# A recurrent layer on one core: four groups of seven transposed by DMA instead of three, with a shared reciprocal square root and copies split between two engines

## The chip, the cores and the metric

The kernel runs on one core of a Trainium2 chip. The metric is the device time of one execution in microseconds. Five instruction streams work side by side: TensorE (PE, with its weight loads PEld), VectorE (DVE), ScalarE (ACT), GpSimd (POOL) and SyncE (SP, which here only issues DMAs). Each runs its own instructions in order; between streams they wait on semaphores. L1101 means line 1101 of the kernel.

## The reference

Two layers over 3327 nodes with 256 features, each a graph attention followed by a feed-forward part. Layer 0 has a two-head attention and a mixture of 16 experts. Layer 1 has a one-head attention and the part that matters here, a recurrence of 30 steps over all rows:

```python
def step(h, _):
    h = h + 0.01 * jnp.tanh(h)
    h = h * jax.nn.sigmoid(h)
    h = _layernorm(h, ln_w, ln_b)
    h = jnp.einsum('bsc,dc->bsd', h, W) + b
    return (h, None)
x, _ = jax.lax.scan(step, x, None, length=N_ITERS)     # N_ITERS = 30
```

`_layernorm` subtracts the mean of a row, multiplies by 1/sqrt(variance + 1e-5) and applies `ln_w` and `ln_b`. Rows don't depend on each other, steps do.

## The kernel before

Rows are held in 26 tiles of 128 rows, features along the free dimension, in one SBUF tensor `x`. Two attentions, the experts and the second attention come first (about 1080 us); the change is in the recurrence behind them.

**Groups.** The 26 tiles make seven groups (`COUNT`): positions 0 to 5 have four tiles, position 6 has two. 30 steps of seven groups are 210 groups, numbered by `at`; the position is `at % 7`. As seven is odd, a position has an even number in one step and an odd one in the next. Within one step the groups are independent; group `at` needs what group `at - 7` has left in `x`.

**Stages of a group**, each a method of `Group`:

- `tanh` (L1046, ScalarE): `th = tanh(hs / 100)`; `hs` is the group's part of `x`, scaled by 100.
- `add` (L1049, GpSimd): `th = th + hs`.
- `silu` (L1053, ScalarE): `z = silu(th / 100)`.
- `measure` (L1058, L1061, VectorE): mean and variance of every row of `z`, by `bn_stats` and `bn_aggr`, one instruction a tile.
- `invert` (L1066, L1067, GpSimd): variance plus epsilon, then to the power -0.5. The mean is never subtracted from `z`; it has been taken out of the weights `wc` beforehand.
- The transpose of `z`, since the product contracts over features. There are two ways. `turn_here`: TensorE transposes 128 x 128 blocks into PSUM (L1077, eight for a group of four tiles) and ScalarE copies them to SBUF (L1079, two for a group of four tiles). `turn_away`: ScalarE splits every float into its two 16-bit halves (L1086, one copy for the group), a DMA writes these to a DRAM buffer `apart` (L1087), and a DMA of the transposing kind reads them back turned (L1091). Both DMAs are issued by SP. The positions in `AWAY = (1, 3, 5)` go this way.
- `product` (L1101, TensorE): `po = zT x wc`, 16 matrix products in two passes by four tiles, into one of two PSUM buffers `po`.
- `evict` (L1111, VectorE): `hs = po * r + bb`, one instruction a tile; `r` is the result of `invert`. In the last step it also adds the layer's input (L1119, with `old`, loaded back from DRAM by SP) and writes the output.

**Order.** The order is written out by hand, a software pipeline: iteration `at` works on groups of different ages, and `put` keeps the instructions of each engine in that order from the second step on. The loop is

```python
on(at - 1, Group.evict)
on(at + 3, Group.invert)
on(at + 4, Group.silu)
on(at + 2, lambda g: g.away or g.turn_here())
on(at + 4, lambda g: g.away and g.turn_away())
on(at + 4, Group.measure)
on(at + 6, Group.tanh)
on(at + 5, Group.add)
on(at, Group.product)
```

So on TensorE, an iteration is the transposes of the group two ahead (if it is turned there) and then a product; on VectorE, the eviction of the group behind and then the measurement of the group four ahead; on GpSimd, an inversion and an addition; on ScalarE, `silu`, copies, `tanh`. A group's state goes round in seven iterations: `evict` and the next step's `tanh` in one, `add` in the next, `silu` in the one after that, and the product four iterations later.

**Buffers.** `po` has two (a product waits until the group two before it has been evicted). `wide` tiles (`th`, `z`) have four, `narrow` ones eight. The halves and the transposed result of `turn_away` use buffers of the pool `steps`, two each, and `apart` has two.

Of the kernel before, what the change touches and what calls it, by code (L numbers as in the profile page):

```python
# [11 lines left out]
F32 = mybir.dt.float32  # L12
I32 = mybir.dt.int32
I16 = mybir.dt.int16
BF16 = mybir.dt.bfloat16
FP8 = mybir.dt.float8e4
AF = mybir.ActivationFunctionType
ALU = mybir.AluOpType
# [3 lines left out]
P = 128  # L22
ALPHA = 0.2
EPS = 1e-5
N_STEPS = 30
S = 100.0
G = 4
MOST = 6
# [3 lines left out]
def gat_moe_gat_recurrent_ffn(ctx: ExitStack, tc: tile.TileContext, a: dict, out: bass.AP):  # L32
    nc = tc.nc
    N, D = a["x"].shape
    KD = D // P
    NT = (N + P - 1) // P
    NP = NT * P
    PAIRS = NT // 2
# [25 lines left out]
    const = ctx.enter_context(tc.tile_pool(name="const", bufs=1))  # L64
# [32 lines left out]

    ident = const.tile([P, P], F32, name="ident")
    make_identity(nc, ident)
    neg_half = const.tile([P, MOST], F32, name="neg_half")  # L100
    nc.vector.memset(neg_half, -0.5)


# [80 lines left out]
    class Scores:  # L184


        def __init__(self, pool, heads, s=None):
            self.s = pool.tile([P, NT, 2, heads], F32, name="s") if s is None else s
            self.row = pool.tile([P, NT, heads], F32, name="row")
            self.full = pool.tile([P, NT, heads], F32, name="full")  # L190
            self.part = pool.tile([P, NT, heads], F32, name="part")
            self.minus = pool.tile([P, NT, heads], F32, name="minus")
# [113 lines left out]
    graph = ctx.enter_context(tc.tile_pool(name="graph", bufs=1))  # L306
    adj_pairs = graph.tile([P, PAIRS, NP], BF16, name="adjT")
    adjT = adj_pairs.bitcast(FP8).rearrange("p c (i b) -> p c i b", b=2)
# [37 lines left out]
    dram = ctx.enter_context(tc.tile_pool(name="dram", bufs=1, space=bass.MemoryType.DRAM))  # L346
# [35 lines left out]
    with ExitStack() as moe:  # L382
# [542 lines left out]
        bb = rec.tile([P, D], F32, name="bb")  # L925
# [18 lines left out]
    steps = ctx.enter_context(tc.tile_pool(name="steps", bufs=2))  # L944
# [73 lines left out]
    with ExitStack() as st:  # L1018
        ps_t = st.enter_context(tc.tile_pool(name="ps3t", bufs=2, space=PSUM))
        turns = cycle((ps, ps_t))  # L1020
        ps_o = st.enter_context(tc.tile_pool(name="ps3o", bufs=2, space=PSUM))
        last_p = st.enter_context(tc.tile_pool(name="last", bufs=2))

        apart = [dram.tile([G * P, 2, D], I16, name=f"apart{q}") for q in range(2)]
        wide = st.enter_context(tc.tile_pool(name="wide", bufs=4))
        narrow = st.enter_context(tc.tile_pool(name="narrow", bufs=8))

        AWAY = (1, 3, 5)
        COUNT = len(groups)
        LAST = N_STEPS * COUNT  # L1030

        class Group:

            def __init__(self, at):
                self.at = at
                self.ts = groups[at % COUNT]
                self.n = len(self.ts)
                self.hs = x[:, self.ts[0] : self.ts[0] + self.n, :]
                self.away = at % COUNT in AWAY

            def put(self, ins):
                return tc.keep_in_program_order(ins) if self.at >= COUNT else ins

            def tanh(self):
                self.th = wide.tile([P, G, D], F32, name="wth")[:, : self.n, :]
                self.put(nc.scalar.activation(self.th, self.hs, AF.Tanh, scale=1.0 / S))  # L1046

            def add(self):
                self.put(nc.gpsimd.tensor_tensor(self.th, self.th, self.hs, ALU.add))  # L1049

            def silu(self):
                self.z = wide.tile([P, G, D], F32, name="wz")[:, : self.n, :]
                self.put(nc.scalar.activation(self.z, self.th, AF.Silu, scale=1.0 / S))  # L1053

            def measure(self):
                stats = narrow.tile([P, G, 6], F32, name="stats")
                for j in range(self.n):
                    self.put(nc.vector.bn_stats(stats[:, j, :], self.z[:, j, :]))  # L1058
                self.v = narrow.tile([P, G, 2], F32, name="v")
                for j in range(self.n):  # L1060
                    self.put(nc.vector.bn_aggr(self.v[:, j, :], stats[:, j, :]))  # L1061

            def invert(self):
                self.r = narrow.tile([P, G], F32, name="rr")
                r = self.r[:, : self.n]
                self.put(nc.gpsimd.tensor_scalar(r, self.v[:, : self.n, 1], EPS, None, op0=ALU.add))  # L1066
                self.put(nc.gpsimd.tensor_tensor(r, r, neg_half[:, : self.n], ALU.pow))  # L1067

            def turn_here(self):
                pool = next(turns)  # L1070
                zT = steps.tile([P, G, KD, P], F32, name="zT")
                for c in range(self.n // 2):
                    pt = pool.tile([P, 2, KD, P], F32, name="bank")
                    for j in range(2):
                        for k in range(KD):
                            tc.keep_in_program_order(
                                nc.tensor.transpose(pt[:, j, k, :], self.z[:, 2 * c + j, k * P : (k + 1) * P], ident)  # L1077
                            )
                    self.put(nc.scalar.copy(zT[:, 2 * c : 2 * c + 2, :, :], pt))  # L1079
                self.zT = lambda j, k: zT[:, j, k, :]  # L1080

            def turn_away(self):
                n = self.n
                parts = steps.tile([P, G, 2, D], I16, name="th")[:, :n]
                here = apart[self.at % COUNT // 2 % 2][: n * P]
                self.put(nc.scalar.copy(parts, self.z.bitcast(I16).rearrange("p j (d b) -> p j b d", b=2)))  # L1086
                nc.sync.dma_start(  # L1087
                    here.rearrange("(j p) b d -> p j (b d)", p=P), parts.rearrange("p j b d -> p j (b d)")
                )
                zT = steps.tile([P, KD, G * P], F32, name="z")  # L1090
                nc.sync.dma_start(  # L1091
                    zT.bitcast(I16)[:, :, : n * 2 * P], here.rearrange("t b d -> (t b) d"), transpose=True
                )
                self.zT = lambda j, k: zT[:, k, j * P : (j + 1) * P]

            def product(self):
                self.po = ps_o.tile([P, G, D], F32, name="po")
                for j in range(self.n):
                    for k in range(KD):
                        tc.keep_in_program_order(  # L1100
                            nc.tensor.matmul(  # L1101
                                self.po[:, j, :], lhsT=self.zT(j, k), rhs=wc[:, k, :],
                                start=(k == 0), stop=(k == KD - 1),
                            )
                        )

            def evict(self):
                ts, n = self.ts, self.n
                for j in range(n):
                    self.put(  # L1110
                        nc.vector.scalar_tensor_tensor(  # L1111
                            self.hs[:, j, :], self.po[:, j, :], self.r[:, j : j + 1], bb, op0=ALU.mult, op1=ALU.add
                        )
                    )
                if self.at >= LAST - COUNT:
                    here = slice(ts[0] * P, (ts[-1] + 1) * P)
                    old = last_p.tile([P, G, D], F32, name="old")
                    nc.sync.dma_start(old[:, :n, :], kept[here, :].rearrange("(t p) d -> p t d", p=P))
                    nc.vector.scalar_tensor_tensor(  # L1119
                        self.hs, self.hs, 1.0 / S, old[:, :n, :], op0=ALU.mult, op1=ALU.add  # L1120
                    )
                    move_pairs(out, self.hs, ts[0] // 2, (ts[-1] + 1) // 2, True)

        live = {}

        def on(at, *what):
            if 0 <= at < LAST:
                if at not in live:
                    live[at] = Group(at)
                for w in what:  # L1130
                    w(live[at])

        for at in range(-6, LAST + 2):
            on(at - 1, Group.evict)
            live.pop(at - 1, None)
            on(at + 3, Group.invert)
            on(at + 4, Group.silu)
            on(at + 2, lambda g: g.away or g.turn_here())
            on(at + 4, lambda g: g.away and g.turn_away())
            on(at + 4, Group.measure)  # L1140
            on(at + 6, Group.tanh)
            on(at + 5, Group.add)
            on(at, Group.product)
# [49 lines left out]
```

## Time and profile before

| | us |
|---|---|
| median of 3 runs | 1873.88 (1872.47 to 1874.83) |
| profiled execution, its time | 1875.77 |
| profiled execution, its span | 1874.0 |
| TensorE busy in the span | 1815.3 (97%), mean granted clock 0.992 |
| VectorE, ScalarE, GpSimd busy | 1281.8, 1177.1, 936.9 |

The instructions of the recurrence between 1200 and 1800 us, from the groups by line and shape:

| line | engine | what | mean us of one |
|---|---|---|---|
| L1046 | ScalarE | tanh, four tiles / two | 1.06 / 0.64 |
| L1053 | ScalarE | silu, four tiles / two | 1.05 / 0.62 |
| L1079 | ScalarE | copy of two transposed tiles | 0.58 |
| L1086 | ScalarE | copy of the halves of four tiles | 1.90 |
| L1049 | GpSimd | addition, four tiles / two | 2.37 / 1.28 |
| L1066 | GpSimd | variance plus epsilon | 0.23 |
| L1067 | GpSimd | power, 4 columns / 2 | 1.04 / 0.72 |
| L1058 | VectorE | bn_stats, one tile | 0.41 |
| L1061 | VectorE | bn_aggr, one tile | 0.16 |
| L1111 | VectorE | eviction, one tile | 0.48 |

How to read it: a mean is from an instruction's start to its end, and instructions that follow each other on one engine overlap at their ends, so four of 0.41 us take 1.40. A matmul record shows about 0.38 us, yet sixteen of them take 3.46 us from start to start of what follows; the chain of waits shows these true lengths. "Idle before" is the time that an engine stood still ahead of an instruction, with what ended the wait. In the chain of waits, lines stand in order of time, and only what sets the end is in it.

### The profile page before, as it was taken

How to read it: one execution, taken by the hardware profiler on the slowest of the kernel's cores; microseconds unless marked ns; L12 is line 12 of the kernel's file. 1: busy time of each engine (PE TensorE's matmuls, PEld its weight loads, DVE VectorE, ACT ScalarE, POOL GpSimd, SP SyncE). 2: the span in 40 equal slices, each digit the busy share in tenths (PEclk: the TensorE clock that was granted, in tenths of full speed). 3: DMA queues.
4: the chain of work that ended last, by engine and by line, in shares of the span. 5: the costliest groups of instructions: out<-in, count | busy, mean ns of one | idle time of the engine just before them, and what ended most of it. 6: DMA issues, size and time to landing. Idle time of an engine off the chain costs nothing.

```text
span 1874.0 us, 32159 instructions
## 1 busy us (share of the span) xinstructions
PE 1815.3 (97%) x11204; PEld 1658.8 (89%) x11204; DVE 1281.8 (68%) x3829; ACT 1177.1 (63%) x1487; POOL 936.9 (50%) x864
## 2 busy tenths in 40 slices
PE   6999999999999998999999979999999999999997
PEld 6999999998999997788888868888888888888886
DVE  6888888842222222666767678888888888888887
ACT  2877777631111111655555578888888888888884
POOL 3010212255333331100000079999999999999994
PEclk9999999999999999999999989999999999999999
DMA  8887260179999885300000045545554555554556
GB/s 175 113 126 96 53 99 23 59 237 300 344 336 338 298 273 183 106 13 18 22 13 17 16 110 133 124 127 122 124 124 124 124 127 122 125 122 124 124 130 197
DMA packets 379919, 255.04 MB, mean 136 GB/s; under 512 B 240917, under 2 KB 339532, under 8 KB 379754
## 3 DMA queue, kind: packets, MB, share of 16 engines
q1 hardware_dynamic: 363634, 220.08, 43.0%
q0 software_dynamic: 11440, 28.09, 8.6%
q10 hardware_dynamic: 4680, 4.76, 0.8%
q8 instruction: 92, 1.51, 0.3%
q14 instruction: 73, 0.60, 0.1%
HBM read 168.19 MB, written 77.01 MB: 131 GB/s over the span
## 4 chain that ended last, share of the span: by engine, by line
PE 67%; issue 10%; POOL 6%; DVE 5%; DMA 4%; ACT 1%; SPq 0%; POOLq 0%; DVEq 0%; ACTq 0%
PE po L1101 34%; PE acc L286 25%; PE bank L1077 5%; POOL given L855 2%; POOL rb L761 2%; DVE pT L281 2%; DMA given<-wh,to 2%; DMA old<-kept 1%; DMA wh<-in_w_dram 1%; PE bank L835 1%; POOL wth L1049 1%; PE acc L163 1%; PE bank L526 1%; PE bank L148 0%; DMA lists<-pair,ati 0%
## 5 line engine op out<-in xcount | busy, mean ns | idle before, releaser
L276 ACT ACTIVATE e<-rb,minus,full 128x384 f32<-128x384 f32 (+3 forms) x494 | 402.4, 824 | 189.2 <-DVE pT L281 172.4
L1049 POOL TENSOR_TENSOR wth<-wth,x 128x1024 f32<-128x1024 f32 (+1 forms) x210 | 464.8, 2214 | 17.2 <-ACT wth L1046 17.2
L281 DVE SCALAR_TENSOR_TENSOR pT<-e,part,adjT 128x384 f32<-128x384 f32 (+3 forms) x494 | 374.7, 761 | 135.8 <-PE acc L286 120.4
L1111 DVE SCALAR_TENSOR_TENSOR x<-po,rr,bb 128x256 f32<-128x256 f32 x780 | 322.9, 475 | 99.4 <-PE po L1101 63.3
L1101 PE MATMUL po<-wc,zT 128*128 128x256 f32 x1680 | 384.2, 380 | 3.2 <-DVE x L1111 3.2
L1101 PEld LDWEIGHTS po<-wc,zT 128*128 128x128 f32 x1680 | 313.4, 191 | 43.1 <-ACT wz L1053 2.2
L1101 PE MATMUL po<-wc,z 128*128 128x256 f32 x1440 | 325.6, 379 | 0.0
L286 PE MATMUL acc<-wh,pT 128*128 128x129 f32 x2704 | 309.8, 276 | 2.1 <-DVE pT L281 2.1
L286 PEld LDWEIGHTS acc<-wh,pT 128*128 128x128 f32 x2704 | 305.0, 192 | 2.7 <-DVE pT L281 2.5
L1101 PEld LDWEIGHTS po<-wc,z 128*128 128x128 f32 x1440 | 271.3, 190 | 35.7
L286 PE MATMUL acc<-s_wh,pT 128*128 128x257 f32 x1352 | 295.8, 382 | 2.4 <-DVE pT L281 2.4
L286 PEld LDWEIGHTS acc<-s_wh,pT 128*128 128x128 f32 x1352 | 257.6, 191 | 40.4 <-DVE pT L281 3.8
L1058 DVE BATCH_NORM_STATS2 stats<-wz 128x6 f32<-128x256 f32 x780 | 274.4, 413 | 27.5 <-ACT wz L1053 27.3
L1053 ACT ACTIVATE wz<-wth 128x1024 f32<-128x1024 f32 (+1 forms) x210 | 208.0, 990 | 82.7 <-POOL wth L1049 82.4
L121 POOL TENSOR_TENSOR rstd<-ve,neg_half 128x4 f32<-128x4 f32 (+3 forms) x28 | 30.4, 1087 | 441.4 <-DVE ve L119 290.4
L1046 ACT ACTIVATE wth<-x 128x1024 f32<-128x1024 f32 (+1 forms) x210 | 209.8, 999 | 26.7 <-DVE x L1111 22.7
L1067 POOL TENSOR_TENSOR rr<-rr,neg_half 128x4 f32<-128x4 f32 (+1 forms) x210 | 208.2, 992 | 17.5
L1086 ACT COPY th<-wz 128x2048 int16<-128x2048 int16 x90 | 170.9, 1899 | 1.8
L881 ACT ACTIVATE e<-bank 128x512 f32<-128x512 f32 x61 | 36.4, 597 | 196.2 <-PE bank L835 188.8
L885 DVE TENSOR_TENSOR pT<-e,bank 128x512 f32<-128x512 f32 x61 | 41.9, 687 | 166.8 <-PE bank L835 166.7
L835 PEld LDWEIGHTS bank<-hT,wh 128*128 128x128 f32 x1280 | 149.3, 192 | 5.2 <-ACT hT L827 1.4
L835 PE MATMUL bank<-hT,wh 128*128 128x128 f32 x1280 | 150.5, 275 | 2.6 <-DMA wh<-in_w_dram 2.6
(195 smaller groups left out, 1636.3 us busy)
## 6 DMA issues: line engine op xcount, KB each, us to landing
wh<-in_w_dram SPq DMA_DIRECT2D x120, 512.0 KB
apart<-th SPq DMA_DIRECT2D x90, 512.0 KB
first_set<-in_w_dram SPq DMA_DIRECT2D x63, 512.0 KB
in_bytes<-in_adj_dram POOLq DMA_DIRECT2D x3, 2496.0 KB, 28.3
x<-in_x_dram SPq DMA_DIRECT2D x6, 512.0 KB
kept<-x SPq DMA_DIRECT2D x8, 384.0 KB
old<-kept SPq DMA_DIRECT2D x6, 512.0 KB
out_dram<-x SPq DMA_DIRECT2D x6, 512.0 KB
```

The costliest lines, as they stand in the source:

```text
L276: nc.scalar.activation(e[:, : n * P], rb[:, : n * P], AF.Relu, scale=sc.full[:, j, h : h + 1], bias=sc.minus[:, j, h : h + 1],)
L281: masked = nc.vector.scalar_tensor_tensor(pT[:, : n * P], e[:, : n * P], sc.part[:, j, h : h + 1], adjT[:, j // 2, ts[0] * P : (ts[-1] + 1 ...
L286: nc.tensor.matmul(po[c], lhsT=pT[:, c * P : (c + 1) * P], rhs=wh[:, j, h, :], start=(j == 0 and c % per_bank == 0), stop=(j == NT - 1), s ...
L835: nc.tensor.matmul(p[:, f, :], lhsT=w[:, k, f * P : (f + 1) * P], rhs=hT[:, k, :], start=(k == 0), stop=(k == KD - 1),)
L1046: self.put(nc.scalar.activation(self.th, self.hs, AF.Tanh, scale=1.0 / S))
L1049: self.put(nc.gpsimd.tensor_tensor(self.th, self.th, self.hs, ALU.add))
L1053: self.put(nc.scalar.activation(self.z, self.th, AF.Silu, scale=1.0 / S))
L1058: self.put(nc.vector.bn_stats(stats[:, j, :], self.z[:, j, :]))
L1067: self.put(nc.gpsimd.tensor_tensor(r, r, neg_half[:, : self.n], ALU.pow))
L1086: self.put(nc.scalar.copy(parts, self.z.bitcast(I16).rearrange("p j (d b) -> p j b d", b=2)))
L1101: nc.tensor.matmul(self.po[:, j, :], lhsT=self.zT(j, k), rhs=wc[:, k, :], start=(k == 0), stop=(k == KD - 1),)
L1111: nc.vector.scalar_tensor_tensor(self.hs[:, j, :], self.po[:, j, :], self.r[:, j : j + 1], bb, op0=ALU.mult, op1=ALU.add)
```

## The change

- `AWAY` is `(1, 2, 4, 5)`: four positions are turned by DMA, 0, 3 and 6 on TensorE.
- `turn_away` is cut in two. `send_away` makes the halves and writes them to DRAM, at the old place. `take_back` issues the transposing DMA one iteration later; both DMAs are kept in program order, so the write of the next group stands ahead of the transpose of this one on SP's queue.
- In `send_away`, for the odd positions (1 and 5), ScalarE copies the halves of three tiles and VectorE those of the fourth. VectorE's copy stands ahead of the group's measurement.
- `invert` is done for two groups at once, by the odd-numbered one of a pair (`at` even, `at + 1`): one L1066 and one L1067 over the columns of both.
- The buffers of the halves (three) and of the transposed result (five) are cut from the space of the adjacency `adjT`, which the second attention reads last; `apart` has four.

```diff
-    neg_half = const.tile([P, MOST], F32, name="neg_half")
+    neg_half = const.tile([P, 2 * G], F32, name="neg_half")
...
-        apart = [dram.tile([G * P, 2, D], I16, name=f"apart{q}") for q in range(2)]
+        apart = cycle([dram.tile([G * P, 2, D], I16, name=f"apart{q}") for q in range(4)])
+        space = graph.tile([P, PAIRS, NP], BF16, name="adjT").rearrange("p c n -> p (c n)").bitcast(F32)
+        spaces = [space[:, i * G * D : (i + 1) * G * D] for i in range(8)]
+        room_parts, room_back = cycle(spaces[:3]), cycle(spaces[3:])
...
-        AWAY = (1, 3, 5)
+        AWAY = (1, 2, 4, 5)
...
-            def measure(self):
+            def measure(self, other):
+                first = self.at % 2 == 0
+                if first:
+                    self.v = narrow.tile([P, 2 * G, 2], F32, name="v")
+                    self.r = narrow.tile([P, 2 * G], F32, name="rr")
+                    self.c = 0
+                else:
+                    self.v, self.r, self.c = other.v, other.r, other.n
...
             def invert(self):
-                self.r = narrow.tile([P, G], F32, name="rr")
-                r = self.r[:, : self.n]
-                self.put(nc.gpsimd.tensor_scalar(r, self.v[:, : self.n, 1], EPS, None, op0=ALU.add))
-                self.put(nc.gpsimd.tensor_tensor(r, r, neg_half[:, : self.n], ALU.pow))
+                if self.at % 2:
+                    n = self.c + self.n
+                    r = self.r[:, :n]
+                    self.put(nc.gpsimd.tensor_scalar(r, self.v[:, :n, 1], EPS, None, op0=ALU.add))
+                    self.put(nc.gpsimd.tensor_tensor(r, r, neg_half[:, :n], ALU.pow))
...
-            def turn_away(self):
+            def send_away(self):
                 n = self.n
-                parts = steps.tile([P, G, 2, D], I16, name="th")[:, :n]
-                here = apart[self.at % COUNT // 2 % 2][: n * P]
-                self.put(nc.scalar.copy(parts, self.z.bitcast(I16).rearrange("p j (d b) -> p j b d", b=2)))
...
+                halves = self.z.bitcast(I16).rearrange("p j (d b) -> p j b d", b=2)
+                parts = next(room_parts).bitcast(I16).rearrange("p (j b d) -> p j b d", b=2, d=D)[:, :n]
+                self.sent = next(apart)[: n * P]
+                cut = n - self.at % COUNT % 2
+                self.put(nc.scalar.copy(parts[:, :cut], halves[:, :cut]))
+                if cut < n:
+                    self.put(nc.vector.tensor_copy(parts[:, cut:], halves[:, cut:]))
+                tc.keep_in_program_order(
+                    nc.sync.dma_start(
+                        self.sent.rearrange("(j p) b d -> p j (b d)", p=P), parts.rearrange("p j b d -> p j (b d)")
+                    )
+                )
+
+            def take_back(self):
+                back = next(room_back)
+                zT = back.rearrange("p (k t) -> p k t", k=KD)
+                tc.keep_in_program_order(
+                    nc.sync.dma_start(
+                        back.bitcast(I16).rearrange("p (k t) -> p k t", k=KD)[:, :, : self.n * 2 * P], self.sent.rearrange("t b d -> (t b) d"), transpose=True
+                    )
                 )
...
             on(at + 2, lambda g: g.away or g.turn_here())
-            on(at + 4, lambda g: g.away and g.turn_away())
-            on(at + 4, Group.measure)
+            on(at + 4, lambda g: g.away and g.send_away())
+            on(at + 3, lambda g: g.away and g.take_back())
+            on(at + 4, lambda g: g.measure(live.get(g.at - 1)))
```

L1111 reads its column of `r` at `self.c + j`.

More of the change, by code (lines that the diff above doesn't have):

```diff
@@ L1058, in measure @@
                     self.put(nc.vector.bn_stats(stats[:, j, :], self.z[:, j, :]))
-                self.v = narrow.tile([P, G, 2], F32, name="v")
                 for j in range(self.n):
-                    self.put(nc.vector.bn_aggr(self.v[:, j, :], stats[:, j, :]))
+                    self.put(nc.vector.bn_aggr(self.v[:, self.c + j, :], stats[:, j, :]))
             def invert(self):
-                self.r = narrow.tile([P, G], F32, name="rr")
-                r = self.r[:, : self.n]
-                self.put(nc.gpsimd.tensor_scalar(r, self.v[:, : self.n, 1], EPS, None, op0=ALU.add))
-                self.put(nc.gpsimd.tensor_tensor(r, r, neg_half[:, : self.n], ALU.pow))
+                if self.at % 2:
[3 more added lines that the diff above has]
+                    self.put(nc.gpsimd.tensor_tensor(r, r, neg_half[:, :n], ALU.pow))
             def turn_here(self):
@@ L1080, in turn_here @@
                 self.zT = lambda j, k: zT[:, j, k, :]
-            def turn_away(self):
+            def send_away(self):
                 n = self.n
-                parts = steps.tile([P, G, 2, D], I16, name="th")[:, :n]
-                here = apart[self.at % COUNT // 2 % 2][: n * P]
-                self.put(nc.scalar.copy(parts, self.z.bitcast(I16).rearrange("p j (d b) -> p j b d", b=2)))
-                nc.sync.dma_start(
-                    here.rearrange("(j p) b d -> p j (b d)", p=P), parts.rearrange("p j b d -> p j (b d)")
-                )
-                zT = steps.tile([P, KD, G * P], F32, name="z")
-                nc.sync.dma_start(
-                    zT.bitcast(I16)[:, :, : n * 2 * P], here.rearrange("t b d -> (t b) d"), transpose=True
+                halves = self.z.bitcast(I16).rearrange("p j (d b) -> p j b d", b=2)
[9 more added lines that the diff above has]
+                    )
+                )
+            def take_back(self):
[5 more added lines that the diff above has]
+                    )
                 )
@@ L1111, in evict @@
                         nc.vector.scalar_tensor_tensor(
-                            self.hs[:, j, :], self.po[:, j, :], self.r[:, j : j + 1], bb, op0=ALU.mult, op1=ALU.add
+                            self.hs[:, j, :], self.po[:, j, :], self.r[:, self.c + j : self.c + j + 1], bb, op0=ALU.mult, op1=ALU.add
                         )
```

## The prediction

> **What bounds the kernel now.** I read the busy times by stage first, then the chain of waits inside the long stage, then the timeline of one step. The change touches only the recurrence, which fills the last 790 of the 1874.0 us. Busy times of its even part (columns: stretch, length, then busy time of TensorE's matmuls, its weight loads, VectorE, ScalarE, GpSimd, the granted clock, DMA share, GB/s):
>
> ```profile
> 1125.00:1850.00 725.00, 725.00 (x3751) 643.03 (x3751) 605.92 (x2219) 624.51 (x683) 674.08 (x597) 1.00 0.52 125
> ```
>
> TensorE is busy for all of the 725 us at full clock; GpSimd stands at 93%, ScalarE at 86%, VectorE at 84%. The chain of waits says the same. One whole step of it (start, length, line):
>
> ```profile
> 1420.31 0.44 PE bank L1077 x4
> 1420.75 3.46 PE po L1101 x16
> 1424.20 0.87 PE bank L1077 x8
> 1425.08 5.18 PE po L1101 x24
> 1430.26 0.87 PE bank L1077 x8
> 1431.13 6.91 PE po L1101 x32
> 1438.04 0.87 PE bank L1077 x8
> 1438.92 6.91 PE po L1101 x32
> 1445.83 0.44 PE bank L1077 x4
> ```
>
> From one L1077 x4 to the next is 25.52 us, and nothing but TensorE is in it: products (L1101) 22.46 us, transposes (L1077) 3 x 0.87 + 0.44 = 3.05 us. 725 / 25.52 makes 28.4 such steps. I call the groups of a step by their position, 0 to 6; 6 has two tiles.
>
> **Part 1, the transposes of group 2 leave TensorE.** Positions turned on TensorE go from 0, 2, 4, 6 to 0, 3, 6: 8 transposes fewer in a step, 0.87 us. A step would take 24.65 us and 28.4 steps would give 28.4 x 0.87 = 24.7 us.
>
> **Part 2, what the removed turn was covering.** Each product needs one of two PSUM buffers, so group 0's product waits until L1111 has emptied that of group 5, with only the two-tile group 6 between. The timeline there:
>
> ```profile
> 1428.37 1.89 PE L1101 MATMUL po<-wc,zT 128*128 128x256 f32 x8
> 1430.10 1.04 PE L1077 MATMUL bank<-ident,wz 128*128 128x128 f32 x8
> 1430.97 3.62 PE L1101 MATMUL po<-wc,zT 128*128 128x256 f32 x16
> ...
> 1428.64 1.66 DVE L1111 SCALAR_TENSOR_TENSOR x<-po,rr,bb 128x256 f32<-128x256 f32 x4 [1.07 <-PE po L1101]
> ```
>
> The transposes at 1430.10 are group 2's, issued two iterations ahead of their product. Without them TensorE reaches group 0's product at 1430.10, but the buffer is emptied only at 1428.64 + 1.66 = 1430.30. How long after the last L1111 a waiting product starts is seen near the end:
>
> ```profile
> 1862.80 1.97 PE L1101 MATMUL po<-wc,zT 128*128 128x256 f32 x8 [1.42 <-DVE x L1111]
> ...
> 1861.00 1.65 DVE L1111 SCALAR_TENSOR_TENSOR x<-po,rr,bb 128x256 f32<-128x256 f32 x4
> ```
>
> It is released by the last of the four L1111 (1862.65), not the first, and starts 0.15 later. So group 0 starts at about 1430.43: a new gap of 0.33 us in every step. Net 0.87 - 0.33 = 0.54 us a step, 28.4 x 0.54 = 15.3 us. This is the step of the sum I trust most after the 0.87.
>
> **Part 3, ScalarE.** Removed: two L1079 copies, 0.53 each where they run back to back (two take 1.06). Added: one more L1086 copy of 1.90; two of the four shrink to three tiles. From 0.64 us for 512 and 1.06 for 1024 elements (L1046) an instruction is 0.22 + 0.82 per 1000, so 1536 elements take 1.48. Copies go from 3 x 1.90 = 5.70 to 2 x 1.90 + 2 x 1.48 = 6.76: +1.06 - 1.06 = nothing. ScalarE stays at 624.51 / 28.4 = 22.0 of some 25.0 us; TensorE is the cover.
>
> **Part 4, GpSimd.** L1067 takes 0.71 us for 2 and 1.04 for 4 columns, 0.38 + 0.165 a column; so 1.37 for 6, 1.70 for 8. Over two steps 14 of them (13.9 us) and 14 L1066 (3.2) become 7 and 7: 7 x 0.38 + 52 x 0.165 = 11.2, plus 1.6. That is 2.1 us less in a step, GpSimd from 674.08 / 28.4 = 23.7 to 21.6. TensorE bounds, so this saves nothing by itself; it takes away the waits of L1053 for L1049. The factors of an even group now come one iteration later, with two iterations to spare before L1111 uses them.
>
> **Part 5, VectorE's two copies.** No such copy is in the trace. Its own length: at least the 0.29 us of a one-source instruction over 256 elements (L820), at most the 0.69 of a two-source one over 512 (L885); I take 0.50, nearer the one-source row. Two a step: 605.92 / 28.4 = 21.3 becomes 22.3 of 25.0 us, covered by the waits of L1111 for TensorE. But source and target both lie in SBUF, and such instructions have met GpSimd:
>
> ```profile
> 1082.06 4.84 POOL L1049 TENSOR_TENSOR wth<-wth,x 128x1024 f32<-128x1024 f32 x2 [16.33 <-ACT wth L1046]
> 1090.14 2.34 POOL L1049 TENSOR_TENSOR wth<-wth,x 128x1024 f32<-128x1024 f32 x1
> ...
> 1082.48 2.21 DVE L1002 SCALAR_TENSOR_TENSOR high<-low,high 128x256 f32<-128x256 f32 x1
> 1090.69 2.27 DVE L128 TENSOR_SCALAR x<-x,mv,rstd 128x256 f32<-128x256 f32 x2
> ```
>
> L1002 takes 0.41 when GpSimd is idle and L128 0.41; here both end only as the addition L1049 ends. L128 has one tensor source, like the new copy, while bn_stats (L1058) and PSUM readers beside L1049 keep their length. So the copy may wait between 0 and a whole L1049, 2.37 us. VectorE's order then decides who is late: the copy stands ahead of L1058, and that ahead of the next L1111. For group 5 there is slack for 1.8 us or more. For group 1:
>
> ```profile
> 1421.62 2.37 POOL L1049 TENSOR_TENSOR wth<-wth,x 128x1024 f32<-128x1024 f32 x1
> ...
> 1421.99 1.40 DVE L1058 BATCH_NORM_STATS2 stats<-wz 128x6 f32<-128x256 f32 x4
> ```
>
> The copy would start at 1421.99. L1058, L1061 (1.68 us together), group 4's L1111 and group 2's measurements (1.57 + 1.68) bring group 5's L1111 to 1426.92 plus the copy; it starts at 1428.64 now. So up to 1.72 us are hidden, a wait of 1.22; the rest widens the gap of part 2. Where group 0's index is even, its L1066 and L1067 are gone, and L1049 starts at 1420.7 behind the previous one (moved 0.66 by a six-column L1067): a wait of 1.1, hidden. Where it is odd, L1067 grows by 0.33 and L1049 starts at 1421.95, against the copy at 1421.99: a dead heat. Won, it costs nothing; lost, 2.33 + 0.50 - 1.72 = 1.1 us. I take it as won, since the new gap gives GpSimd and ScalarE more room, and keep the loss as a rival.
>
> [...]
>
> **Part 6, DMA order.** A transpose now stands on SP's queue behind the next group's write. Today: write issued at 1405.18, transpose at 1408.17, its traffic from 1409.4 to 1412.0 in the DMA share by half microseconds, the product at 1416.69: 4.7 us to spare. Afterwards group 4's transpose starts about 1.3 later, has group 5's write (1.75 of traffic) ahead, and group 2's missing turn brings the product 0.87 nearer: some 0.8 us remain. Cost zero, with a thin cover; uncovered, up to 1 us in a step. The average DMA share goes from 0.52 to 0.52 x 4/3 x 25.5 / 25.0 = 0.71, so the engines themselves suffice. The new buffers lie in the adjacency's space, whose last reader (L281) ends at 1078.9, ahead of the first copy (1088.85): nothing. In the first step group 1's transpose waits for group 2's copy: between -1 (fewer L1067 on the chain there) and +4 us; I take 2.
>
> **Sum.** 1874.0 - 15.3 + 2 = 1860.7 in the span. That execution took 1875.77 against a median of 1873.88, 1.9 above; scaled to the median, 1861 us. Alone, this case spans 1854 to 1868 (copy's dead heat partly lost, first step's bounds).
>
> **Rivals.** (1) The gap of part 2 does not come: 1873.9 - 24.7 + 2 = 1851. For it: L1111 needs to be only 0.33 earlier. Against: it already starts 0.27 behind the product it waits for. (2) The dead heat is lost in every second step: 28.4 x 0.55 = 15.6 us more, 1877; transposes late by half a microsecond a step end at the same place (14 more, 1875). For it: GpSimd is busy 86% of the time and the cover in part 6 is thin. (3) Slower: group 1's copy loses to L1049 in both kinds of step, 28.4 x 1.1 = 31 us more, 1892. It stalls from a wait of 1.22 and is a net loss from 1.76. Against: in even steps L1049 starts over a microsecond earlier. (4) The change does not do what it says, that is the transposes go and TensorE's step stays at 25.5 for another reason: 1874; the even sums above speak against it.
>
> **How the numbers follow.** Main case 0.47; rival 1, 0.13; rival 2, 0.20; rival 3, 0.15; rival 4, 0.05. A difference under 0.2%, 3.7 us, cannot be told from none. Faster takes the main case, rival 1 and a little of rival 2: 0.64. Same takes half of rivals 2 and 4: 0.14. Slower the rest, 0.22. The range must take rival 1 and most of rival 2: 1848 to 1880.
>
> **What would show it.** Between two x4 transposes about 24.97 us; group 0's product with an idle of 0.3 us put down to L1111; L1067 at 1.4 and 1.7; no product released by a DMA. Copies on VectorE of 0.5 us mean the heat is won, of 2 to 3 us lost. I am wrong if the step is above 25.3, if products wait for the transposes, or if the idle is nowhere.

## The result, and the profile after

| | median us | ratio to before, 95% interval |
|---|---|---|
| before (measured again beside it) | 1875.09 | |
| after | 1891.03 (1889.43 to 1893.44) | 1.0087 (1.0074 to 1.0100) |

The change costs 16 us, where 13 us less was forecast, with a range of 1848 to 1880.

Where it went is read from one landmark, the start of the four transposes of group 6, which come once a step. Before, the first stood at 1113.08 us, the last at 1853.87, the end at 1874.0. After: 1117.82, 1869.74 and 1891.7. So 29 steps took 751.9 us instead of 740.8, **11.1 us more**: 25.93 a step against 25.54. The end behind the last landmark grew from 20.1 to 22.0 us. Of the 4.7 us ahead of the first, 3.4 lie ahead of the recurrence (the second attention's last matrix product starts at 1083.9 instead of 1080.5), in code that the change does not touch; in the other executions profiled here that point lay between 1076.8 and 1088.2.

Busy times of the even part of the changed kernel, in the columns of the first fence of the prediction:

```profile
1125.00:1850.00 725.00, 704.02 (x3469) 607.93 (x3468) 627.22 (x2241) 612.17 (x645) 605.68 (x393) 1.00 0.68 163
```

TensorE is no longer busy all the time: 21 of 725 us are idle. And no other engine is full. GpSimd has fallen from 93% to 84%, VectorE has risen to 87%, ScalarE stands at 84%. With slack on every engine, and the DMA engines at a share of 0.68, what binds is looked for in a chain that runs through several of them; the chain of waits shows it. A whole round of that chain, and of the round before it the addition and a copy on VectorE (start, length, line; L1052 is the addition, L1056 silu, L1068 and L1070 the measurement, L1076 and L1077 the shared inversion, L1100 the copy):

```profile
1401.72 2.34 POOL wth L1052
...
1405.17 1.50 DVE adjT L1100
...
1410.34 2.35 POOL wth L1052
1412.71 1.07 ACT wz L1056
1413.80 1.41 DVE stats L1068 x4
1415.21 0.29 DVE v L1070 x4
1415.50 0.08 issue
1415.58 0.25 POOL rr L1076
1415.90 1.67 POOL rr L1077
1417.57 2.35 POOL wth L1052
```

TensorE is not in it. In an iteration GpSimd's queue holds the inversion first and then an addition. The inversion of a pair waits for the measurement of its odd group; that waits for the group's silu, and that for the group's addition, two additions back on GpSimd itself. So the addition at 1417.57 is late only because it is queued behind an inversion to which it owes nothing. It is **a ring**: 7.23 us for two groups without a copy (1410.34 to 1417.57), 8.62 with a copy that was held (1401.72 to 1410.34). TensorE needs two sevenths of its step, 7.04 us for 24.65 or 7.13 for 24.97.

The additions behind an inversion start, on GpSimd's timeline, at 1401.69, 1410.31 and 1417.54 us, then at

```profile
1425.10 4.68 POOL L1052 TENSOR_TENSOR wth<-wth,x 128x1024 f32<-128x1024 f32 x2
...
1432.01 4.70 POOL L1052 TENSOR_TENSOR wth<-wth,x 128x1024 f32<-128x1024 f32 x2
...
1439.27 4.70 POOL L1052 TENSOR_TENSOR wth<-wth,x 128x1024 f32<-128x1024 f32 x2
...
1446.48 1.28 POOL L1052 TENSOR_TENSOR wth<-wth,x 128x512 f32<-128x512 f32 x1
```

and at 1453.48. So the seven rounds of two steps take 8.62, 7.23, 7.56, 6.91, 7.26, 7.21 and 7.00 us, and from the third step on they repeat to 0.02 us. Together that is 51.8 us, where two steps of 24.97 make 49.9. Of the 1.85 us between, the two copies that stand in the ring make 1.72 (8.62 and 7.56 against 7.23); without them it would be level with TensorE, about 50 us. The last round does not run through GpSimd alone: in the chain of waits, from 1441.66 to 1449.42, copies, tanh and silu in ScalarE's order stand ahead of the next addition.

The waits between 1130 and 1850 us show both joints of the ring (us in total, times, longest), and that neither late transposes nor the new gap of the prediction's part 2 is the main thing:

```profile
ACT wz L1056 <- POOL wth L1052: 104.7, 112, 2.0
POOL rr L1076 <- DVE v L1070: 86.0, 83, 2.0
...
PE po L1122 <- DMA adjT<-apart: 7.6, 12, 1.1
...
PE po L1122 <- DVE x L1132: 3.2, 14, 0.5
```

In the kernel before, over the same stretch:

```profile
POOL rr L1066 <- DVE v L1061: 33.0, 82, 0.6
```

Its ring was there too: 2.37 + 1.06 + 1.70 + 0.31 + 1.04 and some 0.1 of handing over make 6.6 us for two groups, under the 7.29 that two sevenths of 25.52 gave. Sharing the inversion took GpSimd's sum down by 2 us a step and made the ring 0.63 longer, since a power over eight columns stands where one over four stood; taking group 2's transposes from TensorE took the cover down to 7.04.

### The profile page after: what moved, and what is told of

Same layout as the page of the kernel before. It is cut to its first block, busy times and chain, and to the rows that moved or that the text cites. A ratio compares the mean times of both kernels' runs of the same rounds, so it can differ in the third digit from the quotient of the medians.

```text
span 1891.7 us, 31623 instructions
## 1 busy us (share of the span) xinstructions
PE 1806.4 (95%) x10964; PEld 1634.0 (86%) x10964; DVE 1319.3 (70%) x3889; ACT 1173.8 (62%) x1457; POOL 874.6 (46%) x654
## 4 chain that ended last, share of the span: by engine, by line
PE 31%; POOL 25%; DVE 14%; issue 11%; ACT 9%; DMA 4%; SPq 0%; POOLq 0%; DVEq 0%; ACTq 0%
PE acc L286 25%; POOL wth L1052 11%; POOL rr L1077 7%; DVE stats L1068 5%; ACT wz L1056 5%; DMA given<-wh,to 3%; PE po L1122 3%; POOL given L855 2%; POOL rb L761 2%; DVE pT L281 2%; ACT adjT L1098 2%; DVE adjT L1100 2%; DVE v L1070 1%; POOL rr L1076 1%; PE bank L835 1%
## 5 line engine op out<-in xcount | busy, mean ns | idle before, releaser
L1052 POOL TENSOR_TENSOR wth<-wth,x 128x1024 f32<-128x1024 f32 (+1 forms) x210 | 461.7, 2214 | 40.9 <-ACT wth L1049 40.6
L1122 PE MATMUL po<-wc,adjT 128*128 128x256 f32 x1920 | 433.9, 382 | 22.6 <-DMA adjT<-apart 10.2
L1122 PEld LDWEIGHTS po<-wc,adjT 128*128 128x128 f32 x1920 | 358.8, 191 | 76.1 <-DVE stats L1068 15.5
L1068 DVE BATCH_NORM_STATS2 stats<-wz 128x6 f32<-128x256 f32 x780 | 274.5, 412 | 48.1 <-ACT wz L1056 45.1
L1122 PE MATMUL po<-wc,zT 128*128 128x256 f32 x1200 | 279.0, 384 | 11.8 <-ACT zT L1089 6.2
L1056 ACT ACTIVATE wz<-wth 128x1024 f32<-128x1024 f32 (+1 forms) x210 | 208.7, 994 | 114.2 <-POOL wth L1052 112.8
L1122 PEld LDWEIGHTS po<-wc,zT 128*128 128x128 f32 x1200 | 227.0, 192 | 54.1 <-issue 10.0
L1049 ACT ACTIVATE wth<-x 128x1024 f32<-128x1024 f32 (+1 forms) x210 | 209.0, 995 | 10.8 <-DVE x L1132 6.4
L1098 ACT COPY adjT<-wz 128x1536 int16<-128x1536 int16 (+1 forms) x120 | 203.0, 1692 | 0.9
L1077 POOL TENSOR_TENSOR rr<-rr,neg_half 128x8 f32<-128x8 f32 (+1 forms) x105 | 169.4, 1613 | 8.7
```

What stands on the lines that cost most here:

```text
L1077: self.put(nc.gpsimd.tensor_tensor(r, r, neg_half[:, :n], ALU.pow))
L1098: self.put(nc.scalar.copy(parts[:, :cut], halves[:, :cut]))
L1122: nc.tensor.matmul(self.po[:, j, :], lhsT=self.zT(j, k), rhs=wc[:, k, :], start=(k == 0), stop=(k == KD - 1),)
```

## The experiments

Theory A is that ring. Theory B is the prediction's rival 3: VectorE's copies, held by GpSimd's additions, delay the evictions. Theory C: transposes land late behind the next group's write. The step is the mean from the first to the last landmark, the end what follows the last one, both from each run's profile.

| kernel | what differs | ratio to before (95%) | step us | end us |
|---|---|---|---|---|
| before | | 1 | 25.54 | 20.1 |
| after | | 1.0087 (1.0074 to 1.0100) | 25.93 | 22.0 |
| e1_single | after, an inversion for every group | 0.9987 (0.9977 to 0.9996) | 25.35 | 22.8 |
| e2_scalar_copies | after, no copy on VectorE | 1.0109 (1.0092 to 1.0126) | 26.12 | 23.0 |
| e3_add_first | after, addition ahead of inversion | 0.9984 (0.9974 to 0.9994) | 25.27 | 22.8 |
| e4_copy_behind | after, VectorE's copy behind the measurement | 1.0099 (1.0082 to 1.0116) | 25.92 | 21.5 |
| e5_gpsimd_copy | e3, the copy on GpSimd | 0.9964 (0.9950 to 0.9978) | 25.27 | 24.1 |
| e6_before_shared | before, shared inversion alone | 0.9988 (0.9978 to 0.9998) | 25.55 | 18.5 |
| e7_three_po | e3, three product buffers | 0.9989 (0.9978 to 0.9999) | 25.30 | 22.8 |
| e8_early_old | e7, last step's input loaded early | 0.9948 (0.9932 to 0.9965) | 25.27 | 16.5 |
| e9_all | e5, e7 and e8 together | 0.9912 (0.9896 to 0.9929) | 25.16 | 15.6 |
| e10_all_turn_first | e9, transposes ahead of writes | 0.9948 (0.9931 to 0.9965) | 25.47 | 15.7 |
| e11_turn_first | after, transposes ahead of writes | 1.0078 (1.0061 to 1.0095) | 25.96 | 20.8 |
| e12_three_away | after, three groups by DMA again | 1.0059 (1.0042 to 1.0075) | 25.92 | 18.5 |

### Is it the shared inversion? (e1_single)

```diff
             def invert(self):
-                if self.at % 2:
-                    n = self.c + self.n
-                    r = self.r[:, :n]
+                r = self.r[:, : self.n]
```

with `v` and `r` of one group each, as before.

> Only the shared 1/std is undone: every group has its own L1066/L1067 pair again, all else as in the changed kernel. Theory A (a ring through GpSimd's queue: the addition of group k+2 stands behind the inversion of group k, which waits for the measurement of k, which waits for the addition of k; the eight-column power makes two groups' turn 7.24 us and a copy on VectorE in it 7.6 to 8.7, against 7.04 of TensorE): the ring falls to about 6.6 us for two groups, TensorE bounds again at about 25.0 us a step, 1860 to 1870 us. Theory B (the copies on VectorE held by GpSimd's additions delay evictions): as the changed kernel, 1886 to 1895. Theory C (transposes land late behind the next write): as the changed kernel.

Measured: 1875.71 us where before took 1877.99. The loss goes, with this part alone undone, which B and C did not allow. (Only 1 of its 60 copies takes over 1 us, against 16 in the changed kernel, so that this run by itself does not part A from B.) But the step is 25.35 us, not the 25.0 that A expected behind it, and the time lies above A's 1860 to 1870: its chain between 1400 and 1456 us runs through the shorter ring and ScalarE's queue in turn (14.5% of it ScalarE's copies of halves).

### Is it the split? (e2_scalar_copies)

```diff
-                cut = n - self.at % COUNT % 2
+                cut = n
```

> Only the split of two tiles is undone: ScalarE copies all four tiles of groups 1 and 5, VectorE copies nothing. Theory A: the ring loses 0.43 to 1.5 us twice in two steps, but ScalarE has 0.42 us more twice a step, and the eight-column power stays: 1872 to 1886. Theory B: the whole loss goes, 1858 to 1868. Theory C: no change, 1886 to 1895.

Measured: 1898.90 where before took 1877.99, no faster than the changed kernel (the intervals of the two ratios overlap). With no copy on VectorE none can be held, so **theory B falls** as the whole of the loss, unless ScalarE's longer copies cost as much as the held ones did; e3 settles that below. A's number was a miss too, 13 us too low (10, since before was 3 us slower on this chip): it allowed for the copy's way out of the ring but too little for ScalarE, whose in-order stretch of copies, tanh and silu now takes up 13% of the chain between 1400 and 1456 us by L1098 alone, where it took 5% of the changed kernel's between 1400 and 1460. The split gains 0.2 us a step by these two profiles; the times don't show it clearly.

### Is it the order on GpSimd? (e3_add_first)

```diff
-            on(at + 3, Group.invert)
...
             on(at + 5, Group.add)
+            on(at + 3, Group.invert)
```

> GpSimd's order alone is changed: in every iteration the addition stands ahead of the inversion. Theory A: the ring is cut, since no addition waits for a measurement any more; TensorE bounds, 1855 to 1870. Theory B: the copies still meet additions, 1884 to 1895. Theory C: no change.

Measured: 1874.77 where before took 1877.99. Nothing is added, taken out or made shorter here, two calls only change places, and the loss of 0.9% is gone. This is **the run that shows the ring**. An addition still stands behind each inversion, but it is now that of the group three further on, so a round has the time of three groups, and the inversion finds its measurement done: its waits for it, 86.0 us in the changed kernel, are nothing here between 1130 and 1840 us. The steps show what was next. From the third to the last but one they take 24.99 and some 25.45 us in turn. The short ones are the prediction's 24.97. The long ones have this in their chain:

```profile
1448.47 1.26 DVE x L1132 x3
1449.73 2.25 DVE adjT L1100
...
1453.57 1.54 DVE x L1132 x4
```

A copy of 2.25 us between two evictions, where a free one takes 0.43: by its length it is held by an addition, as the prediction feared (earlier in the same trace a copy that starts at 1110.58 takes 1.40 and ends 0.28 behind an addition, 1110.43 + 1.27). With the addition first 43 of 60 such copies take over 1 us (in the changed kernel 16 of 60): more are held, and the loss is gone, which theory B does not allow. The long steps are 0.46 longer than the short ones, where rival 2 priced 1.1. That the held copy makes them long is read from the chain; e5, with no copy on VectorE, has the same mean step and so does not bear it out.

### The copy behind the measurement (e4_copy_behind)

```diff
-            on(at + 4, lambda g: g.away and g.send_away())      # ScalarE's part, VectorE's part, write
+            on(at + 4, lambda g: g.away and g.send_away())      # ScalarE's part
...
             on(at + 4, lambda g: g.measure(live.get(g.at - 1)))
+            on(at + 4, lambda g: g.away and g.write_away())     # VectorE's part, write
```

> VectorE's copy of the fourth tile stands behind the group's measurement instead of ahead of it, and the write with it. Theory A: the ring loses the copy (0.43 to 1.5 us, twice in two steps) but keeps the eight-column power: 1875 to 1886. Theory B: the copy still holds back the next eviction, 1886 to 1895. Theory C: the write leaves some 1.7 us later, so worse: 1895 to 1915.

Measured: 1897.33 where before took 1877.99. The ring has lost its copy and the step stays at 25.92. The rounds show why: those with a copy before now take 7.29 us, but two others have grown, to 8.33 and 7.86. In the chain of waits the first has ScalarE's stretch in it (copies and tanh ahead of silu), the second the copy and a waiting eviction ahead of the next measurement. So taking a copy out of the ring is not enough: ScalarE's order stands right behind it. A expected too much, and the numbers of B and C fit by accident: e2 and e3 exclude B, and products waited 6.7 us for DMAs against 7.6 after the change.

### What still holds e3 (e5_gpsimd_copy, e7_three_po)

```diff
-                    self.put(nc.vector.tensor_copy(parts[:, cut:], halves[:, cut:]))
+                    self.put(nc.gpsimd.tensor_copy(parts[:, cut:], halves[:, cut:]))     # e5, called behind add
...
-        turns = cycle((ps, ps_t))
-        ps_o = st.enter_context(tc.tile_pool(name="ps3o", bufs=2, space=PSUM))
+        turns = cycle((ps,))                                                             # e7
+        ps_o = st.enter_context(tc.tile_pool(name="ps3o", bufs=3, space=PSUM))
```

> As e3_add_first, but the fourth tile's copy is made by GpSimd, right behind its addition, and not by VectorE. With the addition first, steps took 25.0 and 25.46 us in turn (25.23 on the mean), the longer one with a copy of 2.25 us on VectorE held by an addition. Theory B for what is left (the copy is held every second step, the prediction's dead heat): no copy to be held, all steps 25.0, 6 to 7 us under e3, 1866 to 1870. Rival (ScalarE's order of silu, copies and tanh is the limit): 25.2 stays, within 2 us of e3; and if a GpSimd copy takes over 1 us, worse than e3.

> As e3_add_first, but the product has three PSUM buffers instead of two (the transposes use one pool of two banks instead of two pools). The prediction's part 2 (group 0's product waits 0.33 us a step for the eviction of group 5): the gap goes, 0.33 x 29 = 9.6 us under e3, 1863 to 1868, and the short steps take 24.65. Rival (other waits, ScalarE's order above all, are next at the same place): within 3 us of e3.

Measured: e5 1873.53 and e7 1877.09 where before took 1880.37. A copy takes 0.61 us on GpSimd (the median of 60, the longest 1.60), and the shortest of e5's steps take 24.99, but others up to 25.8, so that the mean is e3's, 25.27: theory B's steps of 25.0 throughout did not come. The chain of e5 between 1400 and 1456 us is TensorE, the gap of part 2, and once a transpose that landed late:

```profile
1403.16 1.67 DVE x L1136 x4
1404.83 0.14 issue
1404.97 3.69 PE po L1126 x16
...
1439.55 5.90 DMA adjT<-apart
...
1445.58 3.69 PE po L1126 x16
```

The first three lines are the gap as predicted: the eviction of group 5, 1.67 us, and group 0's product 0.14 behind its end. In e7 the gap is gone (products waited for evictions no more) and the time is the same. Its chain is the held copy again, then ScalarE and GpSimd: a third buffer is worth nothing while these end later. The expectation for e7 was a miss, its rival held.

### The end (e8_early_old)

```diff
-                    old = last_p.tile([P, G, D], F32, name="old")
-                    nc.sync.dma_start(old[:, :n, :], kept[here, :].rearrange("(t p) d -> p t d", p=P))
+                    old = olds[self.at % COUNT].rearrange("p (t d) -> p t d", d=D)       # loaded one step earlier
```

> As e7_three_po, and the layer's input for the last step is loaded one step ahead into free space of the adjacency, so that it no longer stands behind the transposes on SP's queue at the end. The tail from the last small transpose to the end took 22 us after the change and 20 before it, with three loads of some 4 us in its chain: I expect 12 to 14 us, 7 to 10 under e7. Rival (the tail is bound by products and evictions): 2 us or less.

Measured: 1870.31 where before took 1880.37 and e7 1877.09. The end falls from 22.8 to 16.5 us (12 to 14 were expected). In the changed kernel's chain of waits the end is made of these loads, the first of them issued on SP right behind the last transpose (L1111 from 1867.82, 2.92 us):

```profile
1870.79 4.10 DMA old<-kept
...
1876.74 4.49 DMA old<-kept
...
1883.06 4.28 DMA old<-kept
```

### Which parts cost by themselves (e6_before_shared, e12_three_away, e11_turn_first)

e6 is the kernel before with the shared `measure` and `invert`. The other two undo one part of the change:

```diff
-        AWAY = (1, 2, 4, 5)
+        AWAY = (1, 3, 5)                                                 # e12
...
-            on(at + 4, lambda g: g.away and g.send_away())
             on(at + 3, lambda g: g.away and g.take_back())               # e11
+            on(at + 4, lambda g: g.away and g.send_away())
```

> The kernel before with the shared 1/std alone, everything else as before. Theory A: seven pairs make 47.8 us of ring in two steps against 51.0 of TensorE, so the ring is hidden on the mean and costs nothing or little: 1872 to 1880 where before is 1876. Rival (the shared inversion costs by itself, whatever TensorE's step): the after kernel's loss shows here too, 1885 to 1895.

> The changed kernel with only AWAY set back to (1, 3, 5): the fourth group is turned on TensorE again, the pairs, the split (now of three groups) and the order of the DMAs stay. Theory A: TensorE's step is 25.5 again and hides the ring of 7.0 to 7.6 us for two groups (25.5 makes 7.3), mostly: within 0.4% of before. Rival (the pairs and copies cost by themselves): 0.6 to 1.2% slower than before.

> The changed kernel with only that order undone: the transpose of the last group ahead of the write of the next. Theory A: the ring through GpSimd sets the time, so within 4 us of the changed kernel (ratio 1.006 to 1.011). Theory C: 1875 to 1882 where before is 1876.

Measured: e6 1878.08 where before took 1880.37; e12 1885.86 and e11 1889.83 where before took 1874.47. e6's steps are 25.51 or 25.52, all but the first: the longer ring alone is hidden under TensorE's step, as A expects. e12 was a miss for A: its steps are 25.51 and 26.2 in turn. Three copies are made in a step, those of every second step stand in the ring, and two of these are held: 29 of 90. A round with a held one, from addition to addition, in its chain of waits:

```profile
1405.65 2.33 POOL wth L1052
...
1409.10 1.49 DVE adjT L1100
...
1414.26 2.33 POOL wth L1052
```

That is 8.61 us against the 7.29 that TensorE covers. So sharing alone costs nothing; sharing together with copies on VectorE costs 0.6%, also where TensorE has its old length (no product waits for a DMA in e12's steps). e11 stays with the changed kernel: the order of the DMAs is not the cause, and **theory C falls**.

### A version that beats both (e9_all, e10_all_turn_first)

> The changes of e5 (addition first, fourth tile's copy on GpSimd), e7 (three PSUM buffers for the product) and e8 (input of the last step loaded early) together. e5's chain was TensorE, group 0's wait for the eviction of group 5 and now and then a transpose that lands late. With no copy held, the third buffer should be worth its 0.33 us: steps of 24.65 to 24.9 us, 1855 to 1864 where before is 1880. Rival (late transposes take over the place): steps of 25.1 to 25.3, 1866 to 1870, with waits of products for DMA above the 3.2 us of e5.

> As e9_all, but on SP's queue the transpose of the last group stands ahead of the write of the next, as in the kernel before. If the order of writes and transposes makes transposes late (theory C, now in a kernel where nothing hides it), the waits of products for DMA go and 2 to 6 us with them. Rival (the order is harmless or better as changed): the same as e9 or slower.

Measured: e9 1858.31 and e10 1864.88 where before took 1874.47. **e9 is 0.9% faster than the kernel before.** Its gain is only in part what was expected: steps of 24.64 occur, but the mean is 25.16, as a late transpose and ScalarE's stretch still end some of them; the rest of the gain is the end, 15.6 us instead of 20.1. e10 was a miss in a telling direction: with the transpose first on SP's queue, products wait 13.7 us for transposes instead of 4.0, and the chain passes through a write and then its transpose:

```profile
1400.41 3.25 DMA apart<-adjT
...
1403.72 4.32 DMA adjT<-apart
```

The transpose starts 0.06 us behind its write's end, at 1403.66. That the next group's write, which stands behind this transpose on SP's queue, is held back meanwhile is an inference; no row shows it. In this version the order that the change brings is the better one (25.16 us a step against 25.47); behind the ring (e11) it makes no difference that can be seen.

## Why the prediction was wrong, point by point

- **The bound before** was right, and so was that part 1 takes 0.87 us of TensorE's work from a step.
- **Part 2, the gap**, was right in place and size: steps of 24.99 us in e3 against 24.97 worked out, and the rows of e5. (1430.30 + 0.15 is 1430.45, so its own numbers make the gap 0.35 and the step 25.00.) It is 0.33 us of the loss of the full gain, and it stays unseen while something else is later.
- **Part 3** was right: 1.48 us for three tiles, ScalarE at 21.9 us a step of its own (22.0 predicted). e2 shows how little room that leaves.
- **Part 4 is the step that failed.** Its sums were right: powers of 1.67 and 1.35 us (1.70 and 1.37), GpSimd at 21.7 us a step (21.6). "TensorE bounds, so this saves nothing by itself" compared GpSimd's sum with TensorE's step and went no further. The price of an instruction on a queue was taken as its length; what stands behind it, the next addition, and what it waits for, a measurement that hangs on an earlier addition, were not followed round. The ring was in the trace of before, at 6.6 us for two groups, and the numbers of part 4 make it 7.2. With TensorE at 7.04 to 7.13, it could have been forecast that nothing is left to cover it. The size needs the copies as well: the rounds of two steps add up to 51.8 us against 2 x 24.97 predicted, and 1.72 of that is copies in the ring. Nor did sharing take away the waits of L1053 for L1049, as part 4 has it: between 1130 and 1850 us silu waited 104.7 us for additions, 74.4 before.
- **Part 5** was right about when copies are held, and failed with part 4 on what that costs. Their own length is 0.39 to 0.43 us (0.50 taken). Of the 16 held in the changed kernel 14 are group 1's where group 0's index is even, at 1.36 to 1.50 us: the wait of 1.1 that the prediction worked out. Where it is odd, all are free: the dead heat was won. But "a wait of 1.1, hidden" looked at the next evictions alone. The copy stands ahead of a measurement that an inversion waits for, in the ring, and there nothing hides it: 8.62 us against 7.23.
- **Part 6** was right on the average: no loss from the order of the DMAs (e11), a DMA share of 0.68 (0.71). "No product released by a DMA" was not: 12 were, 7.6 us in 720, and in e9 they are among what is left.
- **Rival 3** stood at 1892, and the time is 1891. That is a coincidence of size: its mechanism, copies that lose in every step, is not there: group 1's copy is held in every second step, and e3 has more held copies without the loss.
- **The span's other terms**: the start of the recurrence cost 1.4 us (2 taken, from the attention's last product to the landmark), the end 1.9 (0 taken; loads of the layer's input fill its chain in both kernels, and why they end later was not traced).

How copies fared beside GpSimd's instructions, in the changed kernel: the 44 that start outside additions, or in the last 0.12 us of one, take 0.39 to 0.43 us; the 16 that start 1.07 to 1.22 us ahead of an addition's end last until 0.28 or 0.29 behind it. In e3 the longest takes 2.34 us. bn_stats, with one source, takes at most 0.43 in both kernels. The power holds no copy: 29 of the 60 copies run wholly inside one, at 0.41 to 0.43 us, and that power takes 0.11 to 0.14 longer (1.78 instead of 1.67 with eight columns). These lengths say what one instruction waits, not whether the chain runs through it, and here the second question decided.

What stays open: how ScalarE's order would have to be changed for steps of 24.65 us, which occur in e7 and e9, to become the rule (not tried), and what the loss would be with a ring that holds neither a copy nor any of ScalarE's stretch beside TensorE's shorter step, which no run has.

## What to carry to other kernels

Before an engine with slack is called covered, follow each instruction that is added, merged or moved on its in-order queue once round: what it waits for, what is queued behind it, and whether the two meet again. Such a ring has a length of its own, to be compared with the bounding engine's time for the same number of groups; merging two small instructions into one longer one can shorten an engine's sum (here GpSimd's, by 2 us a step) and lengthen the ring (by 0.63 us for two groups). Where the operation behind a wait doesn't need what is waited for, putting it in front is the first thing to try; here it took 0.66 us off a step, though more copies were held by it.

## What the runs showed that was not expected

- GpSimd copies 512 16-bit elements a partition, with a step of two, in 0.61 us (the median in e5); VectorE in 0.39 to 0.43 and, held, up to 2.34 in e3 and 2.60 in e12. Moving the copy to the slower engine (e5 against e3) left the mean step at 25.27 us.
- The held copy in the long steps of e3 is 1.8 us longer than a free one (2.25 against 0.43 in its chain), yet a long step of e3 only 0.46 longer than a short one. Where the rest goes was not traced.
- In code that no edit touched, ahead of the recurrence, the last matrix product started between 1076.8 and 1088.2 us in the fourteen profiled executions on different chips, which is as much as most effects here; step lengths within one trace agree to 0.01 us in e6 behind its first, and carry the comparison better than single spans.
